# Three edits to the tail of a two-layer kernel: order and banks in routing, row layout of the experts' second weight

## The chip, the cores and the metric

The kernel runs on one core of a Trainium2 chip. The metric is the device time of one execution in microseconds; of the kernel before there are three runs, 10580.3, 10592.63 and 10608.76 us, with a median of 10592.63 us. One further execution was taken with the hardware profiler; all durations come from that one.

The core's engines work side by side and meet through semaphores: TensorE (PE, with its weight loads shown apart as PEld), VectorE (DVE), ScalarE (ACT), GpSimd (POOL) and SyncE (SP), which here only issues DMAs.

## The reference

The input is a batch of 16 images of 128 channels and 64 x 64 pixels, hence 4096 tokens an image. Layer 0 is a selective state-space block on normalised tokens; layer 1 has a causal attention with running maxima and then a mixture of experts in which each expert picks tokens. The change touches the mixture alone:

```python
logits = jnp.einsum('bsd,ed->bse', x, gate_w) + gate_b       # x: layer-normed tokens, E = 64 experts
probs = jax.nn.softmax(logits, axis=1)                        # over the 4096 tokens
vals, idx = jax.lax.top_k(probs.transpose(0, 2, 1), K)        # K = 8 tokens per expert
pooled = jnp.einsum('bked,bke->bed', gathered, topv)          # weighted sum of the chosen tokens
h = gelu(concat(pooled, 1) @ weight1[e])                      # 129 x 512 per expert
out = concat(h, 1) @ weight2[e]                               # 513 x 128 per expert
outputs[chosen tokens] += out * topv
```

All arithmetic is in float32.

## The kernel before, in words

Four stages follow one another. The first computes both the state-space block and the attention, in blocks of 512 tokens, and takes most of the time. Then come routing, the experts and the combination.

**Routing** works on pairs of images: 2 x 64 experts fill the 128 partitions. A pair has eight blocks of 512 tokens per image, so there are 64 iterations, written out by one loop. Every engine's instructions stay in program order there (`InOrder`, line 31 in the profile, is the helper through which all go, so the profile shows line 31 for all of routing and tiles tell the steps apart). One iteration `it` does, in this order:

- `load_tokens(it + 5)`: SP loads two tiles `t` of later tokens.
- `turn(it)`: PE transposes eight 128 x 128 pieces into `x_ps`, two banks wide, double-buffered.
- `shifts`, `scale_logits` (of it - 1): DVE makes `nm`, minus mean times scale, and `ls`, the logits times the scale `rs`.
- `turn_logits(it - 1)`: PE transposes `ls` in four pieces into a bank named `s_ps`; ACT adds the bias and evicts it to the pair's logits `lg`.
- `normed(it - 1)`: ACT writes eight normed tiles `xn` from `x_ps` with `rs` and `nm`.
- `logits(it)`, `stats(it)`: PE multiplies tokens by the gate (`l_ps`), DVE takes means and variances (`mv`) from `x_ps`.
- `largest_of(it - 1)`: after every second block DVE takes the eight largest of two blocks' logits (`top`).
- `choose`, in four parts in iterations 1 to 4 of the next pair: the threshold and a replacing pass `rep` on DVE, an exponential `g` on ACT, a comparing pass, two halves of a masking pass, and the store of `g`.
- `turn_chosen(it - 12)`: PE transposes `g` into an `s_ps` bank, ACT copies it to `gT`.
- `scales(it)`: ACT makes `rs` in two small activations.
- `pool_chosen(it - 13)`: PE accumulates chosen tokens in `pl` over a pair; at a pair's end ACT copies it (`pls`).
- `turn_pooled`: once a pair, PE transposes that into a bank of its own (`plt`), and DVE copies it to `pooled`.

`s_ps` comes from a pool with one bank, through `bank()` (line 955). [...] four for `x_ps`, one each for `l_ps`, `s_ps`, `pl` and `plt`.

**Experts** go in 16 groups of four. Here the framework's scheduler orders the work. SP loads `w1` as one DMA and `w2` as four per group (lines 1151, 1154), with four buffers each. PE multiplies pooled tokens by `w1` (`hps`, 1157) and adds the bias (1160); ACT applies the gelu (`hs`, 1162); PE transposes `hs` in four pieces (`tps`, 1165); DVE copies it (`ht`, 1167); PE multiplies by `w2` (`ops`, 1171) and adds the bias (1174); DVE copies (1176), and ACT's queue stores `o_d` (1178). Partition p of `w2` holds rows p, 128 + p, 256 + p and 384 + p of an expert's matrix, each 512 bytes long.

**The combination** multiplies the experts' outputs by the sparse weights `g` and adds them to the tokens (1197, 1198).

Of the kernel before, what the change touches and what calls it, by code (L numbers as in the profile page):

```python
# [8 lines left out]
F32 = mybir.dt.float32  # L9
# [3 lines left out]
PSUM = bass.MemoryType.PSUM  # L13
DRAM = bass.MemoryType.DRAM

P = 128
L = 512
# [16 lines left out]
def bc(ap, shape):  # L34

    return ap.to_broadcast(list(shape))
# [3 lines left out]
def conv_attn_hybrid(ctx: ExitStack, tc: tile.TileContext, x, w_in, conv_w, conv_b, w_xproj, w_dt, b_dt,  # L40
                     a_log, d_param, w_out, w_kv, q_proj, gate_w, gate_b, weight1, weight2, out):
    nc = tc.nc
# [12 lines left out]
    HID = weight1.shape[2]  # L55
    NHB = HID // P
# [14 lines left out]
    ident = const.tile([P, P], F32, name="ident")  # L71
# [9 lines left out]
    with ExitStack() as st:  # L81
        wp = st.enter_context(tc.tile_pool(name="wp", bufs=1))
        ps = st.enter_context(tc.tile_pool(name="ps", bufs=3, space=PSUM))
        acc = st.enter_context(tc.tile_pool(name="acc", bufs=1, space=PSUM))
        yps = st.enter_context(tc.tile_pool(name="yps", bufs=1, space=PSUM))
        bps = st.enter_context(tc.tile_pool(name="bps", bufs=1, space=PSUM))
        PE, DVE, ACT, POOL, SP = (InOrder(tc, e) for e in (nc.tensor, nc.vector, nc.scalar, nc.gpsimd, nc.sync))
# [82 lines left out]
        with tc.tile_pool(name="prep", bufs=1) as prep:  # L170
# [23 lines left out]
            for j, dst in ((0, wk), (1, wv)):  # L194
                for g in range(HD // 4):
                    tp = ps.tile([P, 4, P], F32, tag="ps", name="kvt_ps")
# [27 lines left out]
        def bank(name):  # L224
            return ps.tile([P, L], F32, tag="ps", name=name)
# [713 lines left out]
    pooled = ff.tile([P, E, 32], F32, name="pooled")  # L939
    nc.gpsimd.memset(pooled, 0.0)  # L940
    with ExitStack() as st:
        PE, DVE, ACT, POOL, SP = (InOrder(tc, e) for e in (nc.tensor, nc.vector, nc.scalar, nc.gpsimd, nc.sync))
# [2 lines left out]
        AHEAD = 5  # L945
        xps = st.enter_context(tc.tile_pool(name="rxps", bufs=2, space=PSUM))
        lps = st.enter_context(tc.tile_pool(name="rlps", bufs=1, space=PSUM))
        sps = st.enter_context(tc.tile_pool(name="rsps", bufs=1, space=PSUM))
        acc = st.enter_context(tc.tile_pool(name="racc", bufs=1, space=PSUM))
        big = st.enter_context(tc.tile_pool(name="big", bufs=2))  # L950
        tsp = st.enter_context(tc.tile_pool(name="tsp", bufs=12))
# [24 lines left out]
        blk, pair = {}, {}  # L976

        def load_tokens(it):
            p, i = divmod(it, NBLK)
            w = blk[it] = {}  # L980
            w["t"] = [tsp.tile([P, L], F32, tag="t", name="t") for _ in range(2)]
            for j in range(2):
                SP.dma_start(w["t"][j], t2_d[2 * p + j, :, bass.ts(i, L)])

        def turn(it):
            w = blk[it]
            w["x"] = xps.tile([P, CB, 2, P], F32, tag="x", name="x_ps")
            for c in range(CB):
                for j in range(2):
                    PE.transpose(w["x"][:, c, j, :], w["t"][j][:, bass.ts(c, P)], ident)  # L990
# [25 lines left out]
        def shifts(it):  # L1016
            w = blk[it]
            nm = w["nm"] = rp_.tile([P, NG], F32, tag="nm", name="nm", bufs=3)
            DVE.scalar_tensor_tensor(nm, w.pop("mv")[:, :, 0], -1.0, w["rs"], ALU.mult, ALU.mult)

        def scale_logits(it):
            w = blk[it]
            w["ls"] = rp_.tile([P, NG, E], F32, tag="ls", name="ls")
            DVE.tensor_tensor(w["ls"], w.pop("l"), bc(w["rs"].unsqueeze(2), [P, NG, E]), ALU.mult)

        def turn_logits(it):
            p, i = divmod(it, NBLK)
            w = blk[it]
            if i == 0:
                pair[p] = dict(lg=big.tile([P, T], F32, tag="lg", name="lg"),  # L1030
                               top4=rp_.tile([P, NBLK // 2, 8], F32, tag="top4", name="top4"))
            ls = w.pop("ls").rearrange("p g e -> p (g e)")
            lp = bank()
            for c in range(CB):
                PE.transpose(lp[:, c, :], ls[:, bass.ts(c, P)], ident)
            ACT.activation(pair[p]["lg"][:, bass.ts(i, L)], lp.rearrange("p c t -> p (c t)"), AF.Identity, bias=gb)

        def normed(it):
            w = blk[it]
            x, rs, nm = w.pop("x"), w.pop("rs"), w.pop("nm")  # L1040
            xn = w["xn"] = xnp.tile([P, CB, 2, P], F32, tag="xn", name="xn2")
            for g in range(NG):
                ACT.activation(xn[:, g // 2, g % 2, :], x[:, g // 2, g % 2, :], AF.Identity, bias=nm[:, g : g + 1],
                               scale=rs[:, g : g + 1])
# [52 lines left out]
                ACT.copy(ps, pl[:, :P])  # L1097

        def turn_pooled(p):
            tp = acc.tile([P, L], F32, tag="plt", name="plt")  # L1100
            PE.transpose(tp[:, :P], pair.pop(p)["ps"], ident)
            DVE.tensor_copy(pooled[:, :, 2 * p : 2 * p + 2], tp[:, :P].rearrange("p (j e) -> p e j", j=2))

        for it in range(AHEAD):
            load_tokens(it)
        for it in range(NIT + LATE + 2):
            p, i = divmod(it, NBLK)
            if it + AHEAD < NIT:
                load_tokens(it + AHEAD)
            if it < NIT:  # L1110
                turn(it)
            if 0 <= it - 1 < NIT:
                shifts(it - 1)
                scale_logits(it - 1)
                turn_logits(it - 1)
                normed(it - 1)
            if it < NIT:
                logits(it)
                stats(it)
            if 0 <= it - 1 < NIT:  # L1120
                largest_of(it - 1)
            if p and p <= NB // 2 and 1 <= i <= 4:
                choose(p - 1, i - 1)
            if 0 <= it - LATE < NIT:
                turn_chosen(it - LATE)
            if it < NIT:
                scales(it)
            if 0 <= it - LATE - 1 < NIT:
                pool_chosen(it - LATE - 1)
            last, left = divmod(it - LATE - 2, NBLK)  # L1130
            if last >= 0 and left == NBLK - 1:
                turn_pooled(last)
# [4 lines left out]
    with ExitStack() as st:  # L1137
        ps = st.enter_context(tc.tile_pool(name="eps", bufs=2, space=PSUM))
        wpool = st.enter_context(tc.tile_pool(name="ew", bufs=4))
        ep = st.enter_context(tc.tile_pool(name="ep", bufs=1))  # L1140
        hp = st.enter_context(tc.tile_pool(name="hp", bufs=2))
        EG = 4
        b1n = ep.tile([E, HID], F32, name="b1n")
        nc.sync.dma_start(b1n, weight1[:, C, :])
        b2n = ep.tile([E, O], F32, name="b2n")
        nc.sync.dma_start(b2n, weight2[:, HID, :])
        sel = ep.tile([E, E, 32], F32, name="sel")
        nc.vector.tensor_copy(sel, bc(ident[:E, :E].unsqueeze(2), [E, E, 32]))
        for e0 in range(0, E, EG):
            w1 = wpool.tile([P, EG, HID], F32, tag="w1", name="w1")  # L1150
            nc.sync.dma_start(w1, weight1[e0 : e0 + EG, :C, :].rearrange("e c h -> c e h"))
            w2 = wpool.tile([P, EG, NHB, O], F32, tag="w2", name="w2")
            for e in range(EG):
                nc.sync.dma_start(w2[:, e], weight2[e0 + e, :HID, :].rearrange("(k p) o -> p k o", p=P))
            hps = ps.tile([P, HID], F32, tag="hps", name="hps")
            for e in range(EG):
                nc.tensor.matmul(hps[32 * e : 32 * e + 32, :], pooled[:, e0 + e, :], w1[:, e, :], start=True,
                                 stop=False)
            for e in range(EG):
                nc.tensor.matmul(hps[32 * e : 32 * e + 32, :], sel[:, e0 + e, :], b1n, start=False, stop=True)  # L1160
            hs = hp.tile([P, HID], F32, tag="hs", name="hs")
            nc.scalar.activation(hs, hps, AF.Gelu)
            tps = ps.tile([P, NHB, P], F32, tag="tps", name="tps")
            for k in range(NHB):
                nc.tensor.transpose(tps[:, k, :], hs[:, bass.ts(k, P)], ident)
            ht = hp.tile([P, NHB, P], F32, tag="ht", name="ht")
            nc.vector.tensor_copy(ht, tps)
            ops = ps.tile([P, O], F32, tag="ops", name="ops")
            for k in range(NHB):
                for e in range(EG):  # L1170
                    nc.tensor.matmul(ops[32 * e : 32 * e + 32, :], ht[:, k, 32 * e : 32 * e + 32], w2[:, e, k, :],
                                     start=(k == 0), stop=False)
            for e in range(EG):
                nc.tensor.matmul(ops[32 * e : 32 * e + 32, :], sel[:, e0 + e, :], b2n, start=False, stop=True)
            os_ = hp.tile([P, O], F32, tag="os", name="os")
            nc.vector.tensor_copy(os_, ops)
            for e in range(EG):
                nc.scalar.dma_start(o_d[:, e0 + e, :], os_[32 * e : 32 * e + NB, :])


    with ExitStack() as st:
        ps = st.enter_context(tc.tile_pool(name="cps", bufs=4, space=PSUM))
# [43 lines left out]
```

## Time and profile before

| what | us |
|---|---|
| three runs, median (lowest to highest) | 10592.63 (10580.3 to 10608.76) |
| profiled execution, its own time | 10585.55 |
| its span on the core | 10583.8 |
| busy in the span: PE, DVE, ACT, POOL | 9294.7, 9048.4, 7298.5, 7402.2 |
| stretch 9765 to 10188 (routing): PE, DVE, ACT busy of 423 | 331.71, 315.90, 294.47 |
| stretch 10225 to 10362 (experts): PE, DVE, ACT busy of 137 | 98.15, 15.73, 10.84 |

The span is counted from its first instruction. A line of groups names the instruction's output and inputs; "idle before" is the time in which its engine stood still just ahead of it, with what ended that. The waits view adds such times by pair of instructions; the chain follows the work back from the last instruction to whatever released each step.

### The profile page before, as it was taken

How to read it: one execution, taken by the hardware profiler on the slowest of the kernel's cores; microseconds unless marked ns; L12 is line 12 of the kernel's file. 1: busy time of each engine (PE TensorE's matmuls, PEld its weight loads, DVE VectorE, ACT ScalarE, POOL GpSimd, SP SyncE). 2: the span in 40 equal slices, each digit the busy share in tenths (PEclk: the TensorE clock that was granted, in tenths of full speed). 3: DMA queues.
4: the chain of work that ended last, by engine and by line, in shares of the span. 5: the costliest groups of instructions: out<-in, count | busy, mean ns of one | idle time of the engine just before them, and what ended most of it. 6: DMA issues, size and time to landing. Idle time of an engine off the chain costs nothing.

```text
span 10583.8 us, 163130 instructions
## 1 busy us (share of the span) xinstructions
PE 9294.7 (88%) x58461; PEld 5670.1 (54%) x58461; DVE 9048.4 (85%) x9987; ACT 7298.5 (69%) x12924; POOL 7402.2 (70%) x4387
## 2 busy tenths in 40 slices
PE   5679999999999999999999999999999999988775
PEld 3345555555555555555555555555555555555652
DVE  8999999999999999999999999999999999921743
ACT  4567777777777777777777777777777777755740
POOL 7888787778787777878777878877787878810000
PEclk7789999999999999999999999999999999999886
DMA  6676666666666666666666766666666666611348
GB/s 172 172 188 171 179 169 180 165 179 173 162 183 161 183 166 181 173 177 170 170 177 168 185 166 186 170 178 170 176 167 173 178 165 181 161 50 39 110 157 355
DMA packets 889083, 1794.66 MB, mean 170 GB/s; under 512 B 96896, under 2 KB 182544, under 8 KB 881104
## 3 DMA queue, kind: packets, MB, share of 16 engines
q1 hardware_dynamic: 732912, 1414.88, 46.4%
q0 software_dynamic: 73728, 268.47, 12.8%
q10 hardware_dynamic: 81632, 100.88, 3.0%
q8 instruction: 463, 7.59, 0.3%
q14 instruction: 348, 2.85, 0.1%
HBM read 1363.98 MB, written 151.52 MB: 143 GB/s over the span
## 4 chain that ended last, share of the span: by engine, by line
PE 61%; ACT 25%; DVE 5%; issue 4%; DMA 3%; POOL 1%; ACTq 1%; SPq 0%; DVEq 0%; POOLq 0%
PE ao_ps L31 9%; PE v_ps L31 9%; PE k_ps L31 8%; ACT da L31 8%; PE y_ps L31 6%; PE carry_ps L31 4%; PE o_ps L31 4%; PE xs_ps L31 4%; ACT wm L31 3%; ACT L219 3%; PE s_ps L31 3%; PE dbl_ps L31 3%; PE dt_ps L31 2%; DVE h L31 2%; PE z_ps L31 2%
## 5 line engine op out<-in xcount | busy, mean ns | idle before, releaser
L31 POOL TENSOR_TENSOR da<-h,bct 128x1024 f32<-128x1024 f32 x2048 | 6600.5, 3223 | 1815.7 <-DVE h L31 812.8
L31 DVE TENSOR_TENSOR_SCAN h<-da,state,bx 128x512 f32<-128x512 f32 x3584 | 4415.2, 1266 | 169.7 <-DVE bx L31 1.9
L31 DVE TENSOR_TENSOR bx<-du,bct 128x1024 f32<-128x1024 f32 x2048 | 2653.7, 1296 | 160.4 <-DMA bct<-bcs 92.0
L31 ACT ACTIVATE da<-delta,a_neg 128x512 f32<-128x512 f32 x4096 | 2628.0, 716 | 42.6 <-DMA da<-da 42.4
L31 PE MATMUL y_ps<-ident,da 128*128 128x128 f32 x12288 | 1800.4, 302 | 237.5 <-DMA da<-da 129.6
L31 PEld LDWEIGHTS y_ps<-ident,da 128*128 128x128 f32 x12288 | 1575.8, 157 | 659.4 <-issue 375.1
L31 PE MATMUL v_ps<-wv,xn 128*128 128x512 f32 x2048 | 1053.8, 639 | 306.8 <-ACT xc L31 299.0
L31 PE MATMUL ao_ps<-wm,v 128*128 128x128 f32 x8192 | 1055.1, 283 | 180.5 <-ACT wm L31 180.5
L31 PEld LDWEIGHTS ao_ps<-wm,v 128*128 128x128 f32 x8192 | 994.1, 195 | 401.6 <-ACT wm L31 246.3
L31 ACT ACTIVATE v<-v_ps 128x512 f32<-128x512 f32 x1024 | 610.2, 597 | 758.3 <-PE v_ps L31 718.0
L31 PE MATMUL k_ps<-xn,wk 128*128 128x512 f32 x2048 | 942.6, 593 | 0.0
L31 PE MATMUL xs_ps<-xb,wc 128*128 128x512 f32 x2048 | 938.0, 594 | 1.8 <-issue 1.8
L31 PEld LDWEIGHTS v_ps<-wv,xn 128*128 128x128 f32 x2048 | 349.9, 195 | 832.7 <-ACT xc L31 326.7
L31 ACT ACTIVATE wm<-w_ps 128x512 f32<-128x512 f32 x1024 | 552.1, 591 | 340.2 <-PE w_ps L31 338.3
L31 ACT ACTIVATE kt<-k_ps 128x512 f32<-128x512 f32 x1024 | 599.5, 600 | 234.4 <-PE k_ps L31 211.5
L31 DVE TENSOR_TENSOR_SCAN h<-da,bx 128x512 f32<-128x512 f32 x512 | 599.9, 1206 | 25.5 <-ACT da L31 0.5
L31 PEld LDWEIGHTS xs_ps<-xb,wc 128*128 128x128 f32 x2048 | 361.6, 191 | 380.5 <-issue 366.0
L31 PEld LDWEIGHTS k_ps<-xn,wk 128*128 128x128 f32 x2048 | 370.2, 190 | 318.5 <-issue 282.9
L31 POOL COPY state<-h 128x2 f32<-128x2 f32 x1792 | 518.1, 289 | 0.0
L31 POOL DMA_DIRECT2D da<-da x512 | 449.1, 877 | 92.1 <-POOL state L31 35.7
L31 ACT ACT_TABLE_LOAD x395 | 506.8, 1283 | 7.7 <-issue 1.5
L31 ACT ACTIVATE xs<-ao_ps 128x256 f32<-128x256 f32 x256 | 97.5, 381 | 438.3 <-PE ao_ps L31 438.3
(196 smaller groups left out, 10679.1 us busy)
## 6 DMA issues: line engine op xcount, KB each, us to landing
bct<-bcs SPq DMA_DIRECT2D x2048, 512.0 KB
da<-da POOLq DMA_DIRECT2D x512, 512.0 KB, 7.9
xs<-t_d SPq DMA_DIRECT2D x240, 256.0 KB
xs<-in_x_dram SPq DMA_DIRECT2D x128, 256.0 KB
xt<-in_x_dram SPq DMA_DIRECT2D x64, 512.0 KB
t_d<-xt SPq DMA_DIRECT2D x64, 512.0 KB
t_d<-xs ACTq DMA_DIRECT2D x256, 128.0 KB
t<-t_d SPq DMA_DIRECT2D x128, 256.0 KB
```

The costliest lines, as they stand in the source:

```text
L31: return lambda *args, **kw: self.tc.keep_in_program_order(f(*args, **kw))
L219: tc.keep_in_program_order(nc.scalar.preload_act_table_set(EXP_LN))
```

## The change

In routing, `normed(it - 1)` moves ahead of `turn_logits(it - 1)`; only ACT has instructions in `normed`, so only ACT's order changes: eight normed tiles, then the eviction of the logits. The pool of `s_ps` gets two banks. The transposed pooled tokens take a bank of that pool and give up `plt`, so that the sum stays eight.

In the experts, `w2` is loaded with rows 4p to 4p + 3 on partition p: four neighbouring rows, 2048 contiguous bytes. To match, the four transposes of `hs` take every fourth column in place of 128 neighbouring ones. The same numbers are multiplied; their sums over the hidden dimension are formed in another order.

```diff
-        sps = st.enter_context(tc.tile_pool(name="rsps", bufs=1, space=PSUM))
+        sps = st.enter_context(tc.tile_pool(name="rsps", bufs=2, space=PSUM))
...
         def turn_pooled(p):
-            tp = acc.tile([P, L], F32, tag="plt", name="plt")
-            PE.transpose(tp[:, :P], pair.pop(p)["ps"], ident)
-            DVE.tensor_copy(pooled[:, :, 2 * p : 2 * p + 2], tp[:, :P].rearrange("p (j e) -> p e j", j=2))
+            tp = bank()
+            PE.transpose(tp[:, 0, :], pair.pop(p)["ps"], ident)
+            DVE.tensor_copy(pooled[:, :, 2 * p : 2 * p + 2], tp[:, 0, :].rearrange("p (j e) -> p e j", j=2))
...
                 scale_logits(it - 1)
+                normed(it - 1)
                 turn_logits(it - 1)
-                normed(it - 1)
...
-                nc.sync.dma_start(w2[:, e], weight2[e0 + e, :HID, :].rearrange("(k p) o -> p k o", p=P))
+                nc.sync.dma_start(w2[:, e], weight2[e0 + e, :HID, :].rearrange("(p k) o -> p k o", p=P))
...
-                nc.tensor.transpose(tps[:, k, :], hs[:, bass.ts(k, P)], ident)
+                nc.tensor.transpose(tps[:, k, :], hs[:, k::NHB], ident)
```

## The prediction

> **What bounds the kernel now.** I first cut the span into stages with the windows view (columns: stretch, its length, busy time of PE, PEld, DVE, ACT, POOL with counts, granted TensorE clock, DMA share, GB/s). The first 9765 us hold nothing that the change touches; routing takes 460 us, the experts 137 us, the combination 222 us.
>
> ```profile
> 9765.00:10188.00 423.00, 331.71 (x2793) 295.56 (x2793) 315.90 (x1243) 294.47 (x760) 0.00 (x0) 0.88 0.33 112
> 10188.00:10225.00 37.00, 28.12 (x283) 21.96 (x281) 17.64 (x14) 17.22 (x34) 0.00 (x0) 0.82 0.18 65
> 10225.00:10362.00 137.00, 98.15 (x960) 38.26 (x960) 15.73 (x32) 10.84 (x17) 0.00 (x0) 0.68 0.82 249
> 10362.00:10584.00 222.00, 122.36 (x256) 53.88 (x256) 82.79 (x128) 0.00 (x0) 0.00 (x0) 0.68 0.93 380
> ```
>
> In routing no engine is busy over 80% and DMA stands at 0.33: a chain of waits must set the pace. The chain that ended last, over one ordinary block (start, length, what):
>
> ```profile
> 10069.55 0.17 DVE nm L31
> 10069.72 0.61 DVE ls L31
> 10070.33 0.14 issue
> 10070.47 0.64 PE s_ps L31 x4
> 10071.11 0.02 issue
> 10071.13 0.69 ACT lg L31
> 10071.82 2.79 ACT xn L31 x8
> 10074.61 0.48 ACT gT L31
> 10075.09 0.20 ACT rs L31
> 10075.29 0.02 issue
> 10075.32 0.22 ACT rs L31
> ```
>
> The loop closes on ScalarE: rs, then VectorE's nm and ls, then the transposes of the logits, then the eviction lg, and only then the eight normed tiles xn, gT and the next rs: 6.0 us per block, with ACT idle for 1.6. The waits view over 9770:10210 says the same (total us, times, longest):
>
> ```profile
> ACT lg L31 <- PE s_ps L31: 118.5, 63, 4.4
> DVE nm L31 <- ACT rs L31: 87.5, 49, 3.4
> PEld x_ps L31 <- ACT xn L31: 42.7, 56, 2.0
> ```
>
> For the experts I read the same view over 10222:10362:
>
> ```profile
> ACT hs L1162 <- PE hps L1160: 75.6, 10, 8.7
> DVE ht L1167 <- PE tps L1165: 64.5, 15, 5.7
> PE hps L1157 <- DMA w<-in_L_ffn_weight_dram: 7.8, 3, 4.4
> ```
>
> Here ACT and DVE wait for PE, and PE waits little for weights. Starts of hs (10258.71, 10267.17, 10275.22, 10282.83, 10291.29, 10299.37) lie 8.1 us apart, which is a serial chain at low clock: hs 0.6, tps 1.1, ht 0.7, ops 1.9, its bias 0.6, next hps 1.9, its bias 1.9.
>
> [...] after PE's 4.4 us of idling before 10098.17 four s_ps transposes take 1.09 us instead of 0.63. [...] in before each s_ps follows its predecessor's eviction. [...] in 10222:10361 a 512 B packet takes 27 ns at the median (28.7 mean), a 2048 B one 84 ns (97.9), so per byte the small ones are 29% (mean 17%) slower; the measurement decides. [...] The trace has one strided operand, o_ps<-xt at 1035 ns against 592 for o_ps<-z with as many columns: about half streaming rate.
>
> **The change part by part.**
>
> *Normed ahead of the eviction, two banks.* xn needs rs and nm alone. From the chain, ls 0.61, 0.14, s_ps 0.64 and 0.03 leave it: 1.42 us. About 0.03 of hand-over from nm to xn comes in. New ACT loop, counted from nm's start: xn starts at 0.20, lg at 2.99, is done at 3.68, gT 0.48, rs 0.47: 4.63. PE's own loop, start to start: s_ps 0.46, l_ps 1.73, g's transposes 0.54, pl 1.03, x_ps 0.96: 4.72. So an ordinary block takes 4.7, not 6.0. The second bank is what keeps this: g's transposes start at 3.11, before lg has emptied the logits' bank (3.68); with one bank they'd wait, and gT behind them.
>
> What is late next: lg now ends 3.68 after nm, instead of 2.27. In every second block DVE's max of two logit blocks waits for it, and behind it in DVE's queue stand choose's long passes and the next nm. max 1.20 (0.08 overlapping) then ends at 4.80 to 4.88. I write a pair of images as eight blocks, from nm to nm (before: 10063.56 to 10118.16):
>
> - block 5: 5.99 becomes 5.2 (DVE's pooled copy waits for plt, at 4.6 to 4.9 behind pl, then takes 0.29)
> - blocks 6, 7, 0: 6.01, 6.00, 6.01 become 4.85, 4.7, 4.85
> - block 1: 9.69 becomes 8.3 (ACT: lg done, exp 3.69, gT and rs 1.07)
> - block 2: 8.31 becomes 9.2 (max waits to 3.65 behind lg, then 1.12, reciprocal 0.07, the 4.41 pass rep)
> - block 3: 6.41 becomes 5.1 (DVE: 2.81 of nm, ls, statistics, then g 2.33)
> - block 4: 6.18 becomes 7.0 (max behind lg to 4.77, then g 2.25)
>
> Sum 54.6 to 49.2: 5.4 a pair. Five whole pairs (nm 9869.42 to 10142.16) give 27. The last seven intervals (48.6 us) become 44.35: 4. Pair 1 (54.9, without gathers at first) gives 6. The first eight blocks (9768.13 to 9814.49, 46.4 us) alternate 4.2 (ACT without gT) and 4.85 (max), 36.2 with some 2 us of cold start: 8. The end loses: at the last block lg, and with it the final choice, comes after xn instead of before it, 1.4 us; the drain (1.61 us per block: transposes and pl on PE) gains at most 1. Routing: 27+4+6+8-1 = 44 us.
>
> Costing nothing: turn_pooled's use of the shared bank (its predecessor there is lg, done at 3.68, before plt at 4.6); SP's loads, which are five blocks ahead, at 512 KB per 4.7 us or 109 GB/s where the experts draw 249.
>
> *Second weight.* 32768 packets of 512 B become 8192 of 2048 B. Engine time by means: 32768 x 28.7/16 = 58.8 us to 8192 x 97.9/16 = 50.1, 8.7 less; by medians 55.3 to 43.0, 12.3 less. It pays only where the stage waits for weights: PE's 12 us of waits (7.8, and 4.3 on PEld) and the start, where the second group's first weight queues behind it. I take a quarter, 3 us; bounds 0 and 12 us. The 64 transposes now load columns 16 bytes apart. Before doesn't show such a load; between nothing and xt's extra (1035 - 592 ns over 512 columns, so 0.11 us for 128): 0.44 per group of four loads in the serial chain, 7.1 in all. I take half, 3.5. Experts: 0, from 7 slower to 12 faster.
>
> Sum: 44 us off 10585.6, the profiled execution's own time: 10541.6. That execution lies 7 below the median shown (10592.6), whose equivalent is 10548.6. I take 10545, between them; the rivals' times count from 10589 in the same way.
>
> **The rivals.** (1) *The cold clock moves.* Block 1's idle gap shrinks from 4.4 to 3.6 us[...]. If the cold stretch lasts through blocks 2 to 4, where PE needs 8.75 a block (10098.17 to 10106.92), they take 26.2 instead of 21.3: 5 a pair, 30 us or more back; gain 10 to 25, 10564 to 10579. For: pair 1 was cold for 20 us. Against: later pairs came out of it after 10 us of dense work, and the new pace is denser. (2) *Weights were on the path.* The DMA share of 0.82 speaks for it, the waits against; with 12 us from the experts and less stride: gain 58, 10530. (3) *Slower: the strided load.* From 44/64 = 0.69 us more per load on, the whole gain is gone, and slower by 32 us takes 1.2 us a load (10621), ten times xt's extra of 0.11. For: it stands in the serial chain, with nothing beside it. Against: that one measured stride. (4) *Nothing is gained*, because max's wait for lg (lg, max, nm, xn, lg: 0.69+1.12+0.20+2.79 = 4.80) closes a loop as long as the old one: it is 1.2 short of 6.0 (time then 10589).
>
> **How the numbers follow.** Forecast 0.6; rival 1 0.2; rival 2 0.14; rivals 3 and 4 0.06 together, 0.03 each. About 0.3%, 32 us, is what can be told from no change; faster by that means under 10561. Forecast (10530 to 10560) and rival 2 are faster, with a little of rival 1's near end: 0.78; rival 1's rest and rival 4: 0.19; rival 3: 0.03. The range takes in rival 2 and half of rival 1, with 7 us of scatter between runs: 10522 to 10575.
>
> **What would show it.** ACT's wait of lg for s_ps falls from 118.5 us to near nothing; xn directly follows nm; top now waits for lg (some 0.9 us, 31 times); ordinary blocks 4.7 to 4.9 us; the experts still near 137 us with PE waits for weights down; tps loads longer than 142 ns if the stride costs. Wrong if blocks stay at 6.0, if cold stretches outlast 10 us, or if the experts shrink by over 10.

## The result, and the profile after

The changed kernel takes 10547.8 us (median of 20 runs, 10516.8 to 10585.6) beside 10585.4 us (median of 20, 10563.3 to 10608.8) for the kernel before. The ratio is 0.9967, with a 95% interval of 0.9957 to 0.9978: 23 to 46 us faster. The forecast was 10545. The profiled span is 10545.7 us, beside 10583.8.

I cut both profiles at the same events: start, the load of gn that opens routing, the first and the last nm of routing, the load of b1n that opens the experts, the load of on that opens the combination, end.

| stage, us | before | after | difference |
|---|---|---|---|
| first layers (code untouched) | 9756.8 | 9748.6 | -8.2 |
| routing, gn to first nm | 11.3 | 11.0 | -0.3 |
| routing, first to last nm | 422.6 | 388.7 | -33.9 |
| drain of routing, to b1n | 30.9 | 28.8 | -2.1 |
| experts | 140.2 | 134.7 | -5.5 |
| combination (code untouched) | 221.9 | 233.9 | +12.0 |
| span | 10583.8 | 10545.7 | -38.1 |

So the sum came out near the forecast, but its parts did not: routing gave 36 us and not 44, the experts 5.5 and not 0, and two stages that the diff does not touch moved by -8 and +12. These two are one draw: over the fourteen profiles of this document the first layers take 9721.1 to 9766.4 us and the combination 221.8 to 233.9. The windows view of the changed kernel has the same columns as the one shown of before:

```profile
9757.00:10153.00 396.00, 333.66 (x2844) 300.63 (x2845) 319.70 (x1246) 307.14 (x777) 0.00 (x0) 0.88 0.36 119
10153.00:10184.00 31.00, 20.78 (x236) 16.24 (x236) 15.84 (x12) 10.57 (x15) 0.00 (x0) 0.89 0.33 122
10184.00:10320.00 136.00, 93.98 (x960) 37.47 (x952) 15.73 (x32) 10.84 (x17) 0.00 (x0) 0.71 0.77 260
10320.00:10545.00 225.00, 133.91 (x256) 57.74 (x256) 83.47 (x128) 0.00 (x0) 0.00 (x0) 0.64 0.88 364
```

The granted clock (the column after POOL's) is 0.88 in routing as before. In the experts it rose (0.68 to 0.71 in these windows, 0.69 to 0.74 between the events of the table), in the combination it fell (0.68 to 0.64), and the f_ps products there are busy for 133.9 us instead of 122.4, with the same 256 instructions. Keep these clocks in mind for both stages.

One ordinary block of routing, from nm to nm, in the timeline of the changed kernel (start, length, engine, line, what):

```profile
9989.06 0.15 DVE L31 SCALAR_TENSOR_TENSOR nm<-mv,rs 128x8 f32<-128x8 f32 x1
9989.13 0.68 DVE L31 TENSOR_TENSOR ls<-l_ps,rs 128x512 f32<-128x512 f32 x1
9989.25 2.91 ACT L31 ACTIVATE xn<-x_ps,nm,rs 128x128 f32<-128x128 f32 x8 [0.27 <-DVE nm L31]
9989.96 0.63 PE L31 MATMUL s_ps<-ident,ls 128*128 128x128 f32 x4
9992.00 0.72 ACT L31 ACTIVATE lg<-s_ps,gb 128x512 f32<-128x512 f32 x1
9992.15 0.61 PE L31 MATMUL s_ps<-ident,g 128*128 128x128 f32 x4
9992.80 0.59 ACT L31 COPY gT<-s_ps 128x512 f32<-128x512 f32 x1
...
9993.86 0.17 DVE L31 SCALAR_TENSOR_TENSOR nm<-mv,rs 128x8 f32<-128x8 f32 x1 [1.63 <-ACT rs L31]
```

The normed tiles start 0.19 us after nm, while ls and the transposes of the logits run beside them; lg no longer waits for anything. The transposes of g start at 9992.15, before lg ends at 9992.72: the second bank is used. From nm to nm 4.80 us, where it was 6.00. The waits view over 9770:10170 (total us, times, longest) is the counterpart of the one shown of before:

```profile
ACT xn L31 <- DVE nm L31: 57.1, 62, 5.3
DVE nm L31 <- ACT rs L31: 23.4, 20, 2.8
DVE top L31 <- ACT lg L31: 21.2, 27, 2.9
ACT lg L31 <- PE s_ps L31: 0.4, 1, 0.4
```

ACT's wait of lg for PE went from 118.5 us to 0.4, and nm's wait for rs from 87.5 to 23.4. New are 21.2 us in which VectorE's max (top) waits for lg, 27 times.

### The profile page after: what moved, and what is told of

Read it like the earlier page. It is cut to its first block, busy times and chain, and to the rows that moved or that the text cites. A ratio compares the mean times of both kernels' runs of the same rounds, so it can differ in the third digit from the quotient of the medians.

```text
span 10545.7 us, 163123 instructions
## 1 busy us (share of the span) xinstructions
PE 9284.5 (88%) x58461; PEld 5669.1 (54%) x58461; DVE 9040.4 (86%) x9987; ACT 7306.8 (69%) x12924; POOL 7403.4 (70%) x4387
```

## The experiments

**Routing alone, and the second weight alone.** One kernel has the routing edits only, the other the two edits of the second weight only.

```
e1_routing (on before):                      e2_w2 (on before):
 rsps bufs 1 -> 2; turn_pooled uses bank()    "(k p) o -> p k o"  ->  "(p k) o -> p k o"
 normed(it - 1) before turn_logits(it - 1)    hs[:, bass.ts(k, P)]  ->  hs[:, k::NHB]
```

> Both routing edits, the experts as before. Theory (the gain is routing's): from the first nm to the last nm 389 us like the changed kernel (before 422.6), the experts' stage back at 140 us, total 30 to 40 us under before. Rival (the weight's rows carry a good part, by less pressure on the DMA queues): total under 25 us faster, experts' stage 140 and the combination different from both.

> Second weight by four neighbouring rows with strided transposes, routing as before. Theory: routing 422.6 us from first to last nm, experts' stage 135 us instead of 140.3, total 0 to 8 us faster, hardly told from no change. Rival (weights were on the path): 10 us or more faster.

Routing alone: 10544.5 us (16 runs), ratio 0.9965 (0.9953 to 0.9977). The second weight alone: 10574.0 us (14 runs), ratio 0.9996 (0.9984 to 1.0009). In the profiles, first to last nm takes 388.4 us with the routing edits alone (388.7 in the changed kernel) and 426.5 with the weight edits alone. The whole measurable gain is therefore routing's, and the weight edits are worth between 17 us gained and 10 us lost, which cannot be told from nothing. With them alone the experts took 139.2 us, where 135 was expected. Their 426.5 us of routing, where 422.6 was expected, show the scatter: the code of that stage is that of the kernel before, and three more runs with it (e5, e8, e12 below) took 422.8 to 423.1.

**The order alone, the banks alone.** Does the new order need the second bank?

```
e3_order (on before):                     e4_banks (on before):
-                turn_logits(it - 1)       -  tile_pool(name="rsps", bufs=1, ...)
                 normed(it - 1)            +  tile_pool(name="rsps", bufs=2, ...)
+                turn_logits(it - 1)       -  tp = acc.tile([P, L], F32, tag="plt", ...)
                                           +  tp = bank()
```

> Normed tiles ahead of the eviction, but one bank for the turns and plt kept. Theory (the second bank keeps g's transposes from waiting for the logits' eviction): g's transposes start only at 3.7 us after nm, gT at 4.4, so ordinary blocks take 5.4 us instead of 4.8, and first to last nm takes 402 to 408 us. Rival (the bank does not matter): 4.8 and 389 us.

> Two banks for the turns and the shared one for the pooled turn, but the eviction still ahead of the normed tiles. Theory (the bank is not on the old chain): ordinary blocks 6.0 us, first to last nm 421 to 424 us. Rival (the bank alone frees something): under 415 us.

The order alone gives 407.8 us from first to last nm and ordinary blocks of 5.5 us; one run took 10554.3. Where the 0.7 us per block stay is read from its timeline:

```profile
10039.73 0.72 ACT L31 ACTIVATE lg<-s_ps,gb 128x512 f32<-128x512 f32 x1
...
10040.50 0.66 PE L31 MATMUL s_ps<-ident,g 128*128 128x128 f32 x4 [0.47 <-ACT lg L31]
10041.20 0.59 ACT L31 COPY gT<-s_ps 128x512 f32<-128x512 f32 x1 [0.74 <-PE s_ps L31]
```

With one bank the transposes of g wait until lg has emptied it, and then gT waits 0.74 us for them: this is the term that the second bank removes. The banks alone gain nothing (426.2 us, above the 421 to 424 expected and near the 426.5 above, blocks of 5.95; one run 10567.2; its span is 18.3 us shorter than that of before, but its first layers, which no edit touches, are 21.7 shorter). Of the 34 us, the order alone has 15, and the other 19 come only when the second bank is added to it. The two don't add up from their single effects: a second bank has hardly any use while the order puts lg first (5.95 us a block for 6.00).

**The load alone, the strided turns alone.** These split the second weight's edit. In either kernel each hidden value meets another row of the second weight than in the reference, so the output differs; the amount of work does not.

```
e5_load, e12_load (on before):  "(k p) o -> p k o"  ->  "(p k) o -> p k o"
e8_stride (on before):          hs[:, bass.ts(k, P)]  ->  hs[:, k::NHB]
```

> Before, with the second weight alone loaded by four neighbouring rows; hs is still turned in runs of 128 columns, so each hidden value meets another row of the weight (that part of the computation differs). Theory (the load saves some 5 us of waits and the strided turns return a part): experts' stage 133 to 136 us against before's 140.2, PE's waits for weights under 8 us instead of 12. Rival (the load is hidden, the stage follows its chain and TensorE's clock): 138 to 141 us.

> Before, with the strided turns alone and the old load (each hidden value meets another row of the weight; that part differs). Theory (a strided load of 128 columns takes 214 ns instead of 142, which is 0.1 us more from start to start only while the clock is full, nothing while it is halved): experts' stage 140 to 144 us. Rival (the stride is free): 138 to 140.5 us, ht's waits for tps as in before.

The load of the turned columns is dearer. The tile view of tps (weight loads on PE: least, median, most, in ns) of the kernel before, and of the strided turns alone:

```profile
L1165 PEld LDWEIGHTS tps<-ident,hs x64: 138/142/231, 10236.9 to 10355.0; 128*128 128x128 f32 x64
```

```profile
L1165 PEld LDWEIGHTS tps<-ident,hs x64: 195/214/231, 10226.3 to 10347.2; 128*128 128x128 f32 x64
```

The medians lie 0.07 us apart, and both views end at 231 ns: at half clock a load takes 217 ns on average in either layout. How much of this reaches the serial chain is read from the groups of four transposes, which overlap their loads. Two of the kernel before, one at full and one at half clock, and then two of the strided turns:

```profile
10259.36 0.66 PE L1165 MATMUL tps<-ident,hs 128*128 128x128 f32 x4 [1.00 <-ACT hs L1162]
10267.82 1.11 PE L1165 MATMUL tps<-ident,hs 128*128 128x128 f32 x4 [0.78 <-ACT hs L1162]
```

```profile
10254.63 0.75 PE L1165 MATMUL tps<-ident,hs 128*128 128x128 f32 x4 [0.84 <-ACT hs L1162]
10263.18 1.13 PE L1165 MATMUL tps<-ident,hs 128*128 128x128 f32 x4 [0.78 <-ACT hs L1162]
```

So a group is 0.09 us longer at full clock and 0.02 at half, as was expected for this kernel. Over the 16 groups the sum of these lengths goes from 13.4 to 14.8 us: the stride costs 1.3 us, where the prediction took 3.5. The experts took 142.8 us with it, 2.6 more than before, at a clock of 0.68. With the load alone they took 124.8 us, 15 less than before, under both expectations and far more than PE's waits for weights could give back. That looked like rival 2. But the windows view of that stage shows another thing, which made me run the same kernel again:

> The four-row load with unstrided turns once more (each hidden value meets another row of the weight; that part differs). Theory (its 124.8 us of experts came from a full clock, 0.82 against 0.69[...]): experts' stage 128 to 139 us this time. Rival (the load itself saves 15 us): 123 to 127 us again.

The experts' stage in the two runs of this one kernel, first run first:

```profile
10209.50:10334.30 124.80, 86.57 (x993) 34.97 (x993) 17.23 (x34) 11.69 (x19) 0.00 (x0) 0.82 0.81 276
```

```profile
10208.40:10346.50 138.10, 98.59 (x993) 38.44 (x991) 17.20 (x34) 11.69 (x19) 0.00 (x0) 0.71 0.74 249
```

The second run gave 138.1 us at a granted clock of 0.71 where the first had 0.82. The same instructions kept PE busy for 98.6 us instead of 86.6, and 13 us is what the stage differs by. So at least 13 of the 15 us were the clock's and not the load's, and I would have taken them for a result of the edit had I not repeated it. What gives one run the higher clock was not tried. Over the runs that keep this stage's instruction order, its length goes with the granted clock:

| run | e5 | after | e11 | e1 | e6 | e3, e4, e12 | e2 | before | e8 | e7 |
|---|---|---|---|---|---|---|---|---|---|---|
| clock | .82 | .74 | .74 | .73 | .73 | .71 | .70 | .69 | .68 | .62 |
| experts, us | 124.8 | 134.7 | 135.8 | 138.5 | 133.3 | 138.0, 140.6, 138.1 | 139.2 | 140.2 | 142.8 | 147.0 |

A slope of about 11 us per 0.1 of clock, drawn from end to end, comes within 4 us of them all. The effects of the two edits lie within what the clock does to this stage. At clocks of 0.73 and 0.74 the three kernels with both edits (after, e11, e6) took 133.3 to 135.8 us and the one with the old weight (e1) 138.5, so a gain of some us is possible; it is not shown.

**A version with lg in the middle.** If the max's wait for lg is what holds the blocks with choose, then lg between the fourth and the fifth normed tile should end that wait and still leave the logits' transposes covered.

```
e6_split (on after):
-                normed(it - 1)
+                normed(it - 1, 0)        # tiles 0 to 3
                 turn_logits(it - 1)
+                normed(it - 1, 1)        # tiles 4 to 7
```

> The changed kernel with the logits' eviction between the fourth and the fifth normed tile. Theory (max waiting for the late eviction is what costs in blocks 2 and 4 and in every second block): lg ends 2.3 us after nm, block 2 back at 8.3 us, block 4 at 6.2, first to last nm 371 to 377 us against 388.7, total 12 to 18 us under the changed kernel. Rival (PE's loop of 4.7 and its clock set the pace): 384 to 389 us.

First to last nm took 372.6 us, 16.1 less than in the changed kernel. The time is 10523.4 us (6 runs, 10518.7 to 10537.7), ratio to the kernel before 0.9949 (0.9933 to 0.9965). This version beats the kernel before clearly; against the changed kernel it was not timed side by side (0.9967, 0.9957 to 0.9978), so what shows its advantage is the routing stage of the profile, where blocks of one kind repeat to about 0.01 us unless TensorE is at half clock (which still costs this version up to 2 us in single blocks). The block that had cost most, in its timeline:

```profile
9999.79 0.69 ACT L31 ACTIVATE lg<-s_ps,gb 128x512 f32<-128x512 f32 x1
10000.37 1.50 ACT L31 ACTIVATE xn<-x_ps,nm,rs 128x128 f32<-128x128 f32 x4
10000.94 1.19 DVE L31 MAX8 top<-lg 128x8 f32<-128x1024 f32 x1
```

The max starts 0.46 us after lg's end, behind VectorE's own work, and waits for nothing; over the whole stage its wait for lg is 1.6 us, once, instead of 21.2. Block 2 takes 8.32 us instead of 9.25, block 4 6.19 instead of 7.11, and the first eight blocks, after the first two, 4.14 each instead of 4.13 and 4.86 in turn.

**Keeping TensorE busy in the gap.** Some blocks of the changed kernel are slower than their neighbours of the same kind by 2 to 3 us. In this kernel 32 extra transposes of the identity run in each of blocks 1 and 2, where PE idles longest; they add work and leave none out.

```
e7_warm (on after, behind pool_chosen):
+            if p and p <= NB // 2 and 1 <= i <= 2:
+                wp = bank()
+                for c in range(32):
+                    PE.transpose(wp[:, c % CB, :], ident, ident)
```

> The changed kernel with 32 extra transposes of the identity behind the gathers in blocks 1 and 2 of each pair (work added, results unused). Theory (what exceeds 49.5 us a pair is TensorE's half clock after idling): blocks 3, 4 and 5 stay at 5.0, 7.1 and 5.2 in every pair, first to last nm 377 to 382 us. Rival (the extra work itself delays PE): 390 us or more.

It missed: first to last nm 389.6 us, where 377 to 382 was expected; one run 10556.3. Blocks 3 and 4 are now undisturbed in every pair (5.05, and 7.10 to 7.19), and the granted clock in routing is 0.94 instead of 0.88. But block 5 is slow in five pairs, at 6.8 to 8.3 us instead of 5.24. PE in one of these blocks:

```profile
10087.02 0.63 PE L31 MATMUL s_ps<-ident,ls 128*128 128x128 f32 x4 [2.25 <-DVE ls L31]
10087.49 3.25 PE L31 MATMUL l_ps<-gtc,t 128*128 128x64 f32 x16
10090.53 1.06 PE L31 MATMUL s_ps<-ident,g 128*128 128x128 f32 x4
```

The 16 products of l_ps take 3.25 us where a block at full clock has 1.90. With one gap covered, the cold stretches (TensorE at half clock) came at the next one, whose 2.25 us come from VectorE's long pass. The clock that was bought in block 2 bought no time: from pair 2 on that block takes 9.24 to 9.26 us where the changed kernel has 9.24 or 9.25, because there VectorE sets the pace (busy for 8.43 of 9.25 us in a block 2 of the changed kernel).

**The changed kernel once more.** Is it chance where the cold stretches fall?

> The changed kernel once more, beside the split one. Theory[...]: first to last nm 385 to 392 us with the same blocks 1, 2, 6, 7 and 0 but losses in other pairs, experts 132 to 140, combination 222 to 234. Rival (every loss is set by the program): all pieces within 0.5 us of the first profile.

Routing repeated nearly to the hundredth: 388.3 us, with the slow blocks in the same places (8.36 for 8.33, 7.24 and 8.26 for 7.25 and 8.25, 7.76 for 7.83). Against what I expected, they did not move in this run. But the kernel with routing alone (e1) has the same routing code and is a third sample, and it agrees only in part. Counting the first eight blocks as pair 0, pairs 1 to 4 and 7 are as in the other two; in pair 5, however, block 5 is the slow one (7.83 us) and not blocks 3 and 4, and in pair 6, clean in the other two, blocks 3 and 4 take 5.47 and 7.38. So the program does not fix the places. Here is the same gap twice in the first profile of the changed kernel, before block 5 of two different pairs:

```profile
9927.33 0.70 PE L31 MATMUL s_ps<-ident,ls 128*128 128x128 f32 x4 [2.25 <-DVE ls L31]
9927.82 3.52 PE L31 MATMUL l_ps<-gtc,t 128*128 128x64 f32 x16
...
9979.87 0.63 PE L31 MATMUL s_ps<-ident,ls 128*128 128x128 f32 x4 [2.25 <-DVE ls L31]
9980.34 1.90 PE L31 MATMUL l_ps<-gtc,t 128*128 128x64 f32 x16
```

After the same wait of 2.25 us the products take 3.52 us once and 1.90 once. So the length of the gap alone does not decide. The clock records in the traces, which hold when the granted clock changed, say more: in the profiles of the kernel before and of the changed one, each of the 243 and 237 stretches at half clock begins a whole number of steps of 3.413 us after the first one of its profile, to 0.01 us. Half clock here follows a gap of 2.25 us, where the prediction had seen it behind one of 4.4. In the first profile of the changed kernel five such gaps of 2.25 us stand before block 5 in pairs 2 to 7, met at full clock. Two, which end at 9927.33 and 10131.58, lie wholly within one step, and half clock begins at the end of that step (9927.76 and 10132.56). Three, which end at 9877.46, 9979.87 and 10082.13, are cut by the end of a step, with at most 1.48 us in one of the two, and the clock stays full. Of the two shown, the first is whole and the second is cut. Five gaps of one profile do not make this a rule.

Why the places repeat in the second run, and why e1 differs in two pairs all the same, no run here shows.

The rest of that run did differ: combination 226.9 us (233.9), first layers 9721.1 (9748.6). Timed, it took 10538.2 us (6 runs), ratio 0.9960 (0.9940 to 0.9980), which agrees with the first result.

**The experts' chain hidden.** To see whether weights come next once the serial chain is gone: the version with lg in the middle, and with PE doing the next group's first products before this group's turns, and its bias before this group's second products. The second kernel is the same with the old row layout.

```
e9_pipe (on e6_split; experts, PE in order):       e10_pipe_rows (on e9_pipe):
+ for e0 in range(0, E + EG, EG):                  - "(p k) o -> p k o", hs[:, k::NHB]
+     first(e0); turned(e0 - EG)                   + "(k p) o -> p k o", hs[:, bass.ts(k, P)]
+     bias(e0); second(e0 - EG)
```

> The split version, with the experts in a written order on PE: first product of group g, turns of g-1, bias of g, second product of g-1. Theory (the experts' stage is a serial chain and the weights are off the path): with the chain hidden the weights' DMA at some 6.1 us a group (2 x 512 packets of 95 ns over 16 engines) or PE sets the pace, experts' stage 112 to 122 us, total 10 to 22 us under the split version. Rival (TensorE's halved clock sets it, 7.5 us of PE a group): 130 us or more.

> The same with the old row layout (512-byte packets, turns in runs of 128 columns). Theory (once the chain is hidden the packets are on the path): 2048 packets of 28.7 ns in place of 512 of 95 ns make a group's weights 6.8 us, experts' stage 8 to 12 us longer than with four neighbouring rows. Rival (PE's clock sets the pace): within 4 us of it.

The first missed its 112 to 122: the experts took 132.5 us at a clock of 0.72, hardly less than the 133.3 of the version it was built on. That is the rival's number, but the clock is not alone in setting it. It took 10523.9 us (6 runs), ratio 0.9944 (0.9928 to 0.9961), which is that version's time. PE now waits for weights, 13 times, and the queue that issues the loads is itself waiting (PE's row first, then SP's, from the waits view of the stage):

```profile
PE hps L31 <- DMA w<-in_L_ffn_weight_dram: 34.3, 13, 5.9
```

```profile
SPq L1163 <- DMA w<-in_L_ffn_weight_dram: 48.8, 21, 3.7
SPq L1160 <- DMA o_d<-os: 28.9, 12, 4.5
```

So the 12 us of waits for weights that I saw in the kernel before were so small because the chain was slow; with the chain hidden they are 34 us. SP waits for earlier transfers, the stores of o_d among them, before it issues the next load. Which of these it is that sets the pace was not tried. With the old rows this stage takes 139.2 us, 6.7 more, at about the same clock (0.74), and PE waits 41.2 us for weights. That lies between the two expectations (8 to 12, and under 4) and rests on one profile of each (the old rows' run took 10537.2 us), but here the larger packets probably do pay.

## Why the prediction was right, and where it was not

**The loop of an ordinary block: right.** It was to close at 4.7 us with PE's own loop close behind; it takes 4.80 to 4.86. The wait of lg for s_ps did vanish, xn does follow nm, and the max does wait for lg (21.2 us in 27 waits, 0.8 us each; 0.9 us, 31 times was named).

**A pair, block by block: right.** Forecast and measured, in the order 5, 6, 7, 0, 1, 2, 3, 4: 5.2 and 5.24, 4.85 and 4.85, 4.7 and 4.80, 4.85 and 4.86, 8.3 and 8.30, 9.2 and 9.25, 5.1 and 5.05, 7.0 and 7.11. Sum 49.2 and 49.46. The second bank's part, argued from one start (3.11 before 3.68), is what the order alone lacks.

**Routing's total: later stretches at half clock had no term.** I multiplied the clean pair by five. The five whole pairs gave 18.6 us instead of 27, pair 1 4.7 instead of 6, the last seven intervals 1.3 instead of 4, and the first eight 9.4 instead of 8. The blocks that stand above their clean counterparts (7.44, 5.65 and 5.42 in pair 1; then 5.66, 8.33, 7.25 and 8.25, 7.83) add up to 10.7 us. All but 0.4 us of it has TensorE at half clock (in the block of 5.66 us the products take 1.90 us as at full clock, and VectorE's first copy of pooled comes late; no run shows why). The loss is of rival 1's kind, which I had as another case with a chance of 0.2 and 30 us or more: it came beside the forecast and not in its place, at a third of the size, and by another path. Rival 1 let the stretch behind block 1 last through block 4. The gap ahead of that stretch was sized well (3.47 us for 3.6), and in pairs 2 to 6 the stretch ended within block 2, where VectorE sets the pace and it costs nothing. What cost time from there on are second stretches, from block 3 on in one pair and behind the gap before block 5 in two. The argument against rival 1, that the new pace is denser, overlooked that PE still idles 2.25 us there. Of the signs of being wrong, cold stretches of over 10 us, one came, of 17.1 us in pair 1, where the kernel before has one of 20.5; all others in routing are at most 10.24 us, as before. The start and the end of routing together gained 2.4 us where I had the end lose 1, but that cannot be judged: with routing's code unchanged the drain is 28.4 to 28.6 us in four runs (e2, e5, e8, e12) and 30.9 in the kernel before.

**The experts: inside the range, by a term that was missing.** Packets of 2048 B were to save engine time: summed over the packets of 512 and 2048 B in this stage and divided over 16 engines it fell from 111.2 to 101.1 us, between my 8.7 and 12.3. Little of it shows in PE's waits for weights, which stood at 12.1 us and are 11.4: I had taken a saving of 3 us, and 0.7 is what shows. The stride costs 1.3 us where I took 3.5. By these two the stage should have stayed within 1 us of its length, as forecast. It became 5.5 shorter, at a clock of 0.74 instead of 0.69. I had no term for the granted clock of this stage, and it outweighs both edits. The sign of it was in my own list of the chain: its lengths add up to 8.7 us, a group wholly at half clock, where I had read 8.1 us a group.

**The combination: not foreseen.** I counted it as unchanged, since the diff does not touch it. It took 12 us more. The store issues of the changed kernel show where (start, length):

```profile
10442.42 6.38 SPq L1199 DMA_DIRECT2D out_dram<-tc  x2
10469.49 10.75 SPq L1199 DMA_DIRECT2D out_dram<-tc  x2
10500.90 6.16 SPq L1199 DMA_DIRECT2D out_dram<-tc  x2
```

Each line holds the two stores of a pair of images, from the start of the first to the end of the second, and each store waits until VectorE has added up its image (SP's stores wait 123.1 us for VectorE over this stage, in 16 waits). The pairs follow each other every 26 to 28 us, but 31.4 us behind the one whose second store comes 10 us after its first in place of 6. Between these two stores f_ps runs at half clock (0.50 granted over 10472 to 10478). The clock records bear this out. In the kernel before, no half-clock stretch that begins in the stage lasts longer than 17.1 us; in the changed kernel one lasts 27.3 us (10453.41 to 10480.72), and one goes from 10511.44 to the end of the span, 34.2 us. In the other profiles the f_ps products tell the same. In each of the fourteen the shortest takes 589 ns and the longest 1219 or 1220. Their median is 590 ns in the five profiles in which the stage took 221.8 to 222.5 us (before, e2, e4, e7, e8), 693 ns, and 892 in e3, in the six with 226.9 to 229.9 (e1, e3, e5, e6, e9, e11), and 1056 or 1057 ns in the three with 233.2 to 233.9 (e10, e12, the changed kernel). So the 12 us are those of longer stretches at half clock. Among the longer stages are both runs of the load alone, whose routing is that of the kernel before (227.2 and 233.2), so neither the new order in routing nor its pace is needed for it. What makes a stretch long stays open: in these two runs the stores of the first six pairs of images take the same time to 0.02 us, 10.75 and 10.74 us in the fourth among them, and only at the seventh does one have 5.67 us and the other 10.74.

**Rivals.** Rival 2 (weights on the path) needed 12 us from the experts (its 58 us in all are 2 more than 44 and 12 give). With the second weight alone the ratio is 0.9996; its interval reaches to a gain of 17 us, but the experts' stage took 139.2 us for 140.2, and PE's waits for weights fell by 0.7 us only. Something like it shows only once the chain is hidden. Rival 3 needed 0.69 us more per strided load, and 0.07 was measured at full clock, most of it hidden. Rival 4's loop (lg, max, nm, xn, lg) exists, at 4.86 us, and ending it gave another 16 us in the version with lg in the middle.

In short: the mechanism of routing was right, and its gain is the part that repeats, 36 us in both profiles of the changed kernel for 44 forecast. The medians differ by 37.6 us. That the forecast of 10545 came within 3 us of the median is luck: 44 us were too much by 6, and the 10589 from which they were counted lay 4 us above the 10585.4 that the kernel before took in 20 runs. The parts of the first profile that I did not have, -8, -5.5 and +12, are one draw; in the second profile of the same kernel they are -36, -4 and +5.

## What to carry to other kernels

Where an engine's queue holds work that waits and work that could go, write the loop out once for each order, and look for what the later one holds up: of the three places tried here the best for the eviction was neither first nor last but in the middle, where its input is ready and its reader is not yet waiting. An order and the buffer that lets it run belong together, and trying either alone undersells both.

Before a few microseconds of a stage are put down to an edit, look at that stage's granted clock, and run the kernel again if it moved.

## What the runs showed of the hardware that I had not expected

- One and the same kernel had its experts' stage at 124.8 us and at 138.1 us, with the granted clock at 0.82 and 0.71.
- A gap of 2.25 us before the same instruction is followed by half clock at one place and by full clock at another (3.52 and 1.90 us for the same 16 products). The places repeated to about a tenth of a microsecond in a second execution of the kernel, but not all of them in another kernel with the same routing code. In the first profile of the changed kernel both gaps within one step of the clock records were followed by half clock, and none of the three that a step's end cuts.
- In the profiles of the kernel before and of the changed one every stretch at half clock, 243 and 237 of them, begins a whole number of steps of 3.413 us after the first one. The combination's time goes with the clock of its products: 221.8 to 222.5 us where the median f_ps product takes 590 ns, 226.9 to 229.9 where it takes 693 or 892, 233.2 to 233.9 where it takes 1056 or 1057.
- Extra work on an idle TensorE raised its granted clock in routing from 0.88 to 0.94 and saved nothing: the slow stretches came at the next gap.
- A weight load of 128 f32 columns 16 bytes apart takes 214 ns at full clock where adjacent ones take 142, and 217 at half clock either way. A group of four transposes, which overlaps its loads, is 0.09 us longer for it at full clock and 0.02 at half.
